# Moving part of three groups' elementwise work from VectorE to GpSimd in an adaLN layer with spectral attention and experts

## The chip, the core and the metric

The kernel runs on one core of a Trainium2 chip. A core has five engines that work through queues of their own and meet at semaphores: TensorE (PE in the profile; PEld are its weight loads), VectorE (DVE), ScalarE (ACT), GpSimd (POOL) and SyncE (SP), which here only issues transfers. The metric is device time in microseconds from the start to the end of one execution; lower is better. Times of several runs are given as a median with the lowest and the highest.

## The reference, cut to what matters

The input `x` has 4 batches of 1024 tokens with 256 features, so 4096 tokens. Everything is float32.

```
sa, ca, ga, sb, cb, gb = parts of silu(c) @ wmod        # one set for each batch
h = layernorm(x) * (1 + ca) + sa
q, k, v = unit_projection(h @ W.T + b)                  # fft, each bin divided by (|f| + 1e-8), ifft
s = cumsum over the tokens of ifft(fft(k) * fft(v))
x = x + ga * ifft(fft(s) * conj(fft(q)))
h = layernorm(x) * (1 + cb) + sb
x = x + gb * experts(h)                                 # top 2 of 8 experts, SwiGLU, 256 -> 512 -> 256
```

`ga` and `gb` are first pushed away from zero. The experts' weights for a token are a softmax over its two best gate values.

## The kernel before, in words

**Groups and pairs.** Tokens are worked in 8 groups of 512 (`GN`), four tiles of 128 tokens each, two groups to a batch. A group's attention is made in two *pairs* of tiles (the generator `pair`), so the first three groups are six pairs. Spectra are held as 256 real numbers: real parts of the bins, then imaginary parts, with bin 0 and the middle bin at the two ends, which have no imaginary part.

**A pair, step by step.** ScalarE normalizes (L503); TensorE turns the tiles (L510) and makes the spectra of k, v and q with the weights folded into the transform (L526); ScalarE copies them out of PSUM into `z` (L533) and squares them into `sq` (L535, L539). The function `magnitudes` then makes the amplitude of each bin in `mag`: GpSimd copies the two end bins (L545), one engine adds the squares of real and imaginary parts (L549), ScalarE takes the root (L550), VectorE adds EPS (L551). It is called once for k and v together (508 elements a partition, the sum on VectorE) and once for q (254 elements, the sum on GpSimd). VectorE multiplies k's and v's amplitudes (L554) and takes the reciprocal (L555); `complex_product` makes the bin product of k and v by two multiplications (L467, L468) and, for real parts, imaginary parts and the last bin, a subtraction, an addition and a copy (L470, L471, L472); L557 scales it. For q VectorE takes the reciprocal (L560) and GpSimd multiplies (L561). TensorE sums over the tokens (L567, L569, L577) into `pc`, with what the pair before left (`sums`, L585). `complex_product` is called again for `pc`, which lies in PSUM, and q; TensorE turns the result (L592) and transforms it back (L602); VectorE adds it to `x` (L610) and takes the moments (L449, L451). Last, ScalarE normalizes into `row` (L629), and VectorE multiplies by `1 + cb` and adds `sb` (L633, L634).

**A group's routing** (`route`): ranks of the gates (L647 to L652, two of these on GpSimd: L649, L650), softmax weights, the slot of each token (up to L708), eight indirect DMAs from GpSimd's queue that scatter `row` into the experts' slots in DRAM (L713), and the write of `x` with the experts' second bias to `out` (L744). GpSimd then refills the token numbers in `row` (L488), once the scatters have read it.

**Expert blocks.** An expert's slots are worked in blocks of 256 tokens (`Block`): rows and first weights are loaded by SyncE (L857, L864), rows turned (L873), 32 products (L910), the gate part on VectorE (L922), ScalarE (L926, L929), VectorE (L932, L933) and GpSimd (L934; VectorE for the blocks planned after the last group), 16 products (L940), the weighting (L950) and two adding DMAs to `out` from GpSimd's queue (L954). `gb` is fetched by indirect DMAs (L893). A block can be worked only when it is sure to be full; the number that is comes from the shapes (`ready`): none after group 0, one after group 1, four more after each of groups 2 to 6, and 18 of the 39 after the last group. A block's load waits for all scatters so far.

**What sets the order.** A loop over steps at the end (L1036 on) advances the generators in turn: a new pair every four steps, eight steps for each, so that two pairs are always under way; routes after their groups; the preparation of the other batches' constants from step 8 on (`prepare_later`); and parts of expert blocks at a rate that spreads those known over the steps. At build time the framework then orders each engine's instructions once for all, from their dependencies and its own estimate of their durations. On the chip each engine takes them in that order, and one that waits holds those behind it.

Of the kernel before, what the change touches and what calls it, by code (L numbers as in the profile page):

```python
# [10 lines left out]
ALU = mybir.AluOpType  # L11
AX = mybir.AxisListType

P = 128
D = 256
# [2 lines left out]
NF = 512  # L18
GT = 4
GN = GT * P  # L20
LATER = 8
PT = 2
ALPHA = 1.702
# [2 lines left out]
EPS = 1e-8  # L26
# [9 lines left out]
def adaln_layer_kernel(  # L36
# [27 lines left out]
    nc = tc.nc  # L64
    NT = x.shape[0]
    BATCH = c_t.shape[2]
    NG = NT // GN
    GPB = NG // BATCH
# [3 lines left out]
    def ready(n):  # L72

        return max(0, -((NE * (BLK - 1) - 2 * n) // BLK))
# [15 lines left out]
    def bank(tag, bufs=1):  # L90
        return ps_m.tile([P, 512], FP, tag=tag, name=tag, bufs=bufs)
# [6 lines left out]
    def load_x(g):  # L98
        t = xpool.tile([P, GT, D], FP, tag="x", name=f"x{g}")
        nc.sync.dma_start(  # L100
            out=t, in_=x[g * GN : (g + 1) * GN, :].rearrange("(i p) d -> p i d", p=P)
        )
# [72 lines left out]
    SB = LOG + NE  # L175
    CB, GB2 = SB + D, SB + 2 * D
# [277 lines left out]
    def bins(t):  # L454

        return t.rearrange("p k (c n) -> p k c n", c=2)

    def sliding(t, at):

        v = t[:, :, at : at + P]  # L460
        return bass.AP(tensor=v.tensor, offset=v.offset, ap=[*v.ap[:2], (1, 2), v.ap[2]])

    def complex_product(a, b, conj):

        u = two.tile([P, PT, D], FP, tag="u", name="u", bufs=3)
        w = two.tile([P, PT, D], FP, tag="w", name="w")
        nc.vector.tensor_mul(bins(u), bins(a), sliding(b, 0))  # L467
        nc.vector.tensor_mul(bins(w), bins(a), sliding(b, NB))  # L468
        re, im = (ALU.add, ALU.subtract) if conj else (ALU.subtract, ALU.add)
        nc.vector.tensor_tensor(u[:, :, 1:P], u[:, :, 1:P], w[:, :, P : D - 1], re)  # L470
        nc.vector.tensor_tensor(u[:, :, P : D - 1], u[:, :, P : D - 1], w[:, :, 1:P], im)  # L471
        nc.vector.tensor_copy(u[:, :, D - 1 :], w[:, :, D - 1 :])  # L472
        return u

    sums = {}
# [18 lines left out]
    def pair(g, j):  # L494

        b, first = g // GPB, g % GPB == 0
        x4, pb = x_tiles[g], of_batch[b]
        root, r, nmr, gate, row = of_group[g]
        xp = x4[:, j : j + PT, :]
        xn = two.tile([P, PT, D], FP, tag="xn", name="xn")  # L500
        for k in range(PT):
# [19 lines left out]
        mag = two.tile([P, PT, 3, P + 1], FP, tag="mag", name="mag")  # L521
# [16 lines left out]
        k_, v, q = (z[:, :, at : at + D] for at in (KV, KV + D, Q))  # L538
# [1 line left out]
        yield  # L540


        def magnitudes(lo, hi, eng):
            for n in range(2):
                nc.gpsimd.tensor_copy(  # L545
                    mag[:, :, lo:hi, n * P : n * P + 1],
                    sq[:, :, lo:hi, n * (D - 1) : n * (D - 1) + 1],
                )
            eng.tensor_add(mag[:, :, lo:hi, 1:P], sq[:, :, lo:hi, 1:P], sq[:, :, lo:hi, P : D - 1])  # L549
            nc.scalar.activation(mag[:, :, lo:hi, :], mag[:, :, lo:hi, :], AF.Sqrt, bias=tiny)  # L550
            nc.vector.tensor_scalar(mag[:, :, lo:hi, :], mag[:, :, lo:hi, :], EPS, None, ALU.add)  # L551

        magnitudes(1, 3, nc.vector)
        nc.vector.tensor_mul(mag[:, :, 1, :], mag[:, :, 1, :], mag[:, :, 2, :])  # L554
        nc.vector.reciprocal(mag[:, :, 1, :], mag[:, :, 1, :])  # L555
        u = complex_product(k_, v, False)
        nc.vector.tensor_mul(bins(u), bins(u), sliding(mag[:, :, 1, :], 0))  # L557
        yield
        magnitudes(0, 1, nc.gpsimd)
        nc.vector.reciprocal(mag[:, :, 0, :], mag[:, :, 0, :])  # L560
        nc.gpsimd.tensor_mul(bins(q), bins(q), sliding(mag[:, :, 0, :], 0))  # L561
        yield
# [2 lines left out]
        pc = bank("mid").rearrange("p (k n) -> p k n", k=PT)  # L565
# [19 lines left out]
        nc.scalar.copy(sums["s"], pc[:, PT - 1, :])  # L585
        yield

        o = complex_product(pc, q, True)
        pt = bank("mid").rearrange("p (h n) -> p h n", h=2)
        for k in range(PT):  # L590
            for h in range(2):
# [35 lines left out]
        h_row = row[:, j : j + PT, :D]  # L627
        for k in range(PT):
# [1 line left out]
                h_row[:, k, :], xp[:, k, :], AF.Identity,  # L630
                bias=nmr2[:, k : k + 1], scale=r2[:, k : k + 1],
            )
        nc.vector.tensor_mul(h_row, h_row, pb[:, CB : CB + D].unsqueeze(1).to_broadcast([P, PT, D]))  # L633
        nc.vector.tensor_add(h_row, h_row, pb[:, SB : SB + D].unsqueeze(1).to_broadcast([P, PT, D]))  # L634
        yield

    def route(g):
# [90 lines left out]
        for i in range(GT):  # L728
            nc.tensor.transpose(pw[:NE, i * P : (i + 1) * P], wt[:, i, :], ident)
        w_t = one.tile([NE, GN], FP, tag="same", name="w_t")  # L730
        nc.scalar.copy(w_t, pw[:NE, :GN])
        for i in range(0, GT, 2):
# [11 lines left out]
        s = nc.sync.dma_start(  # L744
            out=out[g * GN : (g + 1) * GN, :].rearrange("(i p) d -> p i d", p=P), in_=x4
        )
# [97 lines left out]
    class Block:  # L844
# [24 lines left out]
        def turn(self):  # L869
# [31 lines left out]
            self.h = mtwo.tile([P, NF // P, BLK], FP, tag="h", name="h")  # L901

        def hidden(self, pair):
            ps = []
            for s in range(2):
# [130 lines left out]
    for t in range(NG * PER + STEPS - HALFWAY + 3):  # L1036
        if t < NG * PER and t % PER == 0:
            g = t // PER
# [5 lines left out]
        for r in list(routes):  # L1044
            g, step = r[0], r[1]
            next(r[2])
            r[1] += 1
            if step == 2:
                final = g == NG - 1
                count = TOTAL - ready(GN * g) if final else ready(GN * (g + 1)) - ready(GN * g)  # L1050
                if final:
                    fill_tails()
                if count:
                    planned = plan(count, final)
                    eng = nc.vector if final else nc.gpsimd
# [12 lines left out]
        if t < NG * PER and t % HALFWAY == 0:  # L1068
            n = t // HALFWAY
            new = pair(n // PAIRS, n % PAIRS * PT)  # L1070
            pairs.append([n, 1, new])
            next(new)
        if t >= LATER and t % 2 == 0:
            next(later, None)
# [76 lines left out]
```

## Time and profile before

| | us |
|---|---|
| median of 3 runs (lowest to highest) | 825.14 (820.38 to 828.37) |
| the profiled execution, its own time | 821.18 |
| its span | 819.4 |
| TensorE, matmuls | 709.4 (87% of the span) |
| VectorE | 571.8 (70%) |
| ScalarE | 349.8 (43%) |
| GpSimd | 405.2 (49%) |

The mean granted clock of TensorE is 0.928 of full speed. The profile names a group of instructions by line, engine, operation, and the tiles written and read; `x24` is how often it occurs, then come busy time, the mean duration of one in ns, and the idle time of the engine just before such instructions with what ended it. GpSimd's busy time holds the issue of its indirect DMAs.

The first scatters of the groups 0, 1 and 2 start at 99.9, 142.7 and 199.5 us. GpSimd's own elementwise work is small before: per pair it is the end bins, q's sum and q's scaling.

### The profile page before, as it was taken

How to read it: one execution, taken by the hardware profiler on the slowest of the kernel's cores; microseconds unless marked ns; L12 is line 12 of the kernel's file. 1: busy time of each engine (PE TensorE's matmuls, PEld its weight loads, DVE VectorE, ACT ScalarE, POOL GpSimd, SP SyncE). 2: the span in 40 equal slices, each digit the busy share in tenths (PEclk: the TensorE clock that was granted, in tenths of full speed). 3: DMA queues.
4: the chain of work that ended last, by engine and by line, in shares of the span. 5: the costliest groups of instructions: out<-in, count | busy, mean ns of one | idle time of the engine just before them, and what ended most of it. 6: DMA issues, size and time to landing. Idle time of an engine off the chain costs nothing.

```text
span 819.4 us, 10348 instructions
## 1 busy us (share of the span) xinstructions
PE 709.4 (87%) x2980; PEld 548.9 (67%) x2980; DVE 571.8 (70%) x1599; ACT 349.8 (43%) x632; POOL 405.2 (49%) x399
## 2 busy tenths in 40 slices
PE   6989796597697978997999799979889999999994
PEld 5655553364475756775777577748768888888883
DVE  3688979668668676967696759677846666566552
ACT  3444345264364445645564656364122333322320
POOL 1023243515645663665477446745764545454565
PEclk9999998699699999995999699969979999999998
DMA  9300131520761394228422832284687655666631
GB/s 312 126 0 1 63 143 44 179 75 21 215 181 26 82 294 124 38 70 257 104 35 71 256 81 32 74 253 88 175 251 187 151 163 132 174 164 170 157 52 25
DMA packets 57409, 103.33 MB, mean 126 GB/s; under 512 B 7869, under 2 KB 41802, under 8 KB 56842
## 3 DMA queue, kind: packets, MB, share of 16 engines
q1 hardware_dynamic: 39306, 75.32, 26.8%
q0 software_dynamic: 18048, 27.36, 18.8%
q8 instruction: 25, 0.41, 0.2%
q14 instruction: 30, 0.25, 0.1%
HBM read 75.96 MB, written 28.52 MB: 128 GB/s over the span
## 4 chain that ended last, share of the span: by engine, by line
PE 32%; DVE 16%; DMA 9%; issue 8%; ACT 6%; POOL 3%; POOLq 0%; SPq 0%; ACTq 0%; DVEq 0%
PE gv L910 17%; PE py L940 8%; DMA out_dram<-gb,token 3%; DMA x<-in_x_dram 2%; PE in L526 2%; PE late L735 2%; DVE gt L922 2%; ACT L550 1%; DVE vt L933 1%; DVE vt L932 1%; PE turned L873 1%; POOL slots L713 1%; DMA slots<-row,slot_i 1%; POOL out_dram L954 1%; DMA out_dram<-x 1%
## 5 line engine op out<-in xcount | busy, mean ns | idle before, releaser
L910 PE MATMUL gv<-xt,w 128*128 128x256 f32 x1248 | 301.8, 395 | 18.9 <-DVE gt L922 9.7
L910 PEld LDWEIGHTS gv<-xt,w 128*128 128x128 f32 x1248 | 241.9, 198 | 62.8 <-DVE gt L922 11.4
L954 POOL DMA_INDIRECT out_dram<-gb,token x78 | 130.6, 1675 | 41.8 <-DVE gb L950 20.6
L893 POOL DMA_INDIRECT gb<-kept_gb,token x78 | 83.2, 1067 | 132.2 <-DMA out_dram<-gb,token 29.2
L940 PE MATMUL py<-w_sb,h 128*128 x624 | 142.9, 381 | 6.0 <-POOL h L934 5.1
L940 PEld LDWEIGHTS py<-w_sb,h 128*128 128x128 f32 x624 | 118.1, 191 | 22.9 <-POOL h L934 5.5
L926 ACT ACTIVATE sg<-gt 128x512 f32<-128x512 f32 x78 | 49.1, 630 | 178.9 <-DVE gt L922 169.3
L526 PE MATMUL in<-batch,ht 128*128 128x512 f32 (+1 forms) x256 | 95.6, 520 | 6.1 <-ACT ht L514 6.1
L922 DVE TENSOR_SCALAR gt<-gv,bias 128x256 f32<-128x256 f32 x156 | 68.7, 476 | 35.9 <-PE gv L910 35.9
L713 POOL DMA_INDIRECT slots<-row,slot_i x64 | 68.0, 1063 | 41.8 <-DVE slot_i L708 23.2
L934 POOL TENSOR_TENSOR h<-vt,sg 128x512 f32<-128x512 f32 x42 | 55.5, 1322 | 61.5 <-DVE vt L933 35.1
L526 PEld LDWEIGHTS in<-batch,ht 128*128 128x128 f32 x256 | 48.1, 197 | 43.1 <-issue 30.0
L932 DVE TENSOR_SCALAR vt<-vt 128x512 f32<-128x512 f32 x78 | 37.8, 485 | 48.7 <-ACT vt L929 45.4
L929 ACT ACTIVATE vt<-gv,bias 128x256 f32<-128x256 f32 x156 | 64.9, 465 | 9.7 <-PE gv L910 8.8
L933 DVE TENSOR_TENSOR vt<-vt,gt 128x512 f32<-128x512 f32 x78 | 55.4, 711 | 1.8
L545 POOL COPY mag<-sq 128x4 f32<-128x4 f32 (+1 forms) x64 | 19.0, 336 | 69.7 <-ACT sq L535 57.4
L533 ACT COPY z<-in 128x512 f32<-128x512 f32 (+1 forms) x64 | 29.4, 480 | 46.6 <-PE in L526 43.5
L561 POOL TENSOR_TENSOR z<-z,mag 128x512 f32<-128x512 f32 x16 | 21.0, 1312 | 56.0 <-DVE mag L560 46.2
L950 DVE SCALAR_TENSOR_TENSOR gb<-py,weight,gb 128x256 f32<-128x256 f32 x78 | 34.0, 476 | 15.2 <-PE py L940 15.1
L926 ACT ACT_TABLE_LOAD x25 | 32.1, 1283 | 19.9 <-DVE gt L922 18.1
L551 DVE TENSOR_SCALAR mag<-mag 128x516 f32<-128x516 f32 (+1 forms) x32 | 16.0, 501 | 31.8 <-ACT mag L550 31.8
L550 ACT ACTIVATE mag<-mag,tiny 128x516 f32<-128x516 f32 (+1 forms) x32 | 19.6, 619 | 35.0 <-issue 26.4
(212 smaller groups left out, 1014.8 us busy)
## 6 DMA issues: line engine op xcount, KB each, us to landing
w<-in_w1t_dram SPq DMA_DIRECT2D x39, 1024.0 KB
x_in<-slots SPq DMA_DIRECT2D x39, 266.0 KB
x<-in_x_dram SPq DMA_DIRECT2D x8, 512.0 KB
w_sb<-in_w2t_dram SPq DMA_DIRECT2D x1, 4096.0 KB
out_dram<-x SPq DMA_DIRECT2D x8, 512.0 KB
kept<-of SPq DMA_DIRECT2D x2, 1428.0 KB
batch<-kept SPq DMA_DIRECT2D x2, 1428.0 KB
slots<-fill SPq DMA_DIRECT2D x9, 266.0 KB
```

The costliest lines, as they stand in the source:

```text
L526: nc.tensor.matmul(pz, lhsT=ht[:, h, k * P : (k + 1) * P], rhs=pb[:, h * HC + lo : h * HC + hi], start=(h == 0), stop=(h == 1),)
L713: s = nc.gpsimd.indirect_dma_start(out=slots, out_offset=bass.IndirectOffsetOnAxis(ap=slot_i[:, n, i : i + 1], axis=0), in_=row[:, i, :], ...
L893: nc.gpsimd.indirect_dma_start(out=self.gb[:, i, :], out_offset=None, in_=kept_gb, in_offset=bass.IndirectOffsetOnAxis(ap=self.token[:, i, ...
L910: nc.tensor.matmul(pp[:, j, :], lhsT=self.w1[:, h, s, f * P : (f + 1) * P], rhs=self.xt[:, h, :], start=(h == 0), stop=(h == 1),)
L922: nc.vector.tensor_scalar(gt[:, j], ps[0][:, j], self.bias[:, self.k, 0, f : f + 1], LIMIT, ALU.add, ALU.min)
L926: nc.scalar.activation(sg, gt, AF.Sigmoid, scale=ALPHA)
L929: nc.scalar.activation(vt[:, j], ps[1][:, j], AF.Identity, bias=self.bias[:, self.k, 1, f : f + 1])
L932: nc.vector.tensor_scalar(vt, vt, LIMIT + 1.0, 1.0 - LIMIT, ALU.min, ALU.max)
L933: nc.vector.tensor_mul(vt, vt, gt)
L934: self.eng.tensor_mul(self.h[:, 2 * pair : 2 * pair + 2, :], vt, sg)
L940: nc.tensor.matmul(py[:, i, :], lhsT=self.h[:, f, i * P : (i + 1) * P], rhs=w2_sb[:, bass.ds(self.e, 1), f, :].rearrange("p a d -> p (a d) ...
L954: s = nc.gpsimd.indirect_dma_start(out=out, out_offset=bass.IndirectOffsetOnAxis(ap=self.token[:, i, 0:1], axis=0), in_=y[:, i, :], in_off ...
```

## The change

In groups 0, 1 and 2 (`ALONE = 3`) the engine `side` is GpSimd, in the others VectorE as before. `side` makes the sum of squares for k and v, the EPS addition for q, the last three instructions of the bin product of k and v, and the multiplication and addition after the second normalization. All else keeps its engine: the EPS addition for k and v and the whole product of `pc` and q stay on VectorE. Lines after the edit move by one or two. The order of each engine's instructions is made anew and differs from the old one well past the edited groups.

```diff
+ALONE = 3
...
-    def complex_product(a, b, conj):
+    def complex_product(a, b, conj, eng):
...
-        nc.vector.tensor_tensor(u[:, :, 1:P], u[:, :, 1:P], w[:, :, P : D - 1], re)
-        nc.vector.tensor_tensor(u[:, :, P : D - 1], u[:, :, P : D - 1], w[:, :, 1:P], im)
-        nc.vector.tensor_copy(u[:, :, D - 1 :], w[:, :, D - 1 :])
+        eng.tensor_tensor(u[:, :, 1:P], u[:, :, 1:P], w[:, :, P : D - 1], re)
+        eng.tensor_tensor(u[:, :, P : D - 1], u[:, :, P : D - 1], w[:, :, 1:P], im)
+        eng.tensor_copy(u[:, :, D - 1 :], w[:, :, D - 1 :])
...
+        side = nc.gpsimd if g < ALONE else nc.vector
...
-        def magnitudes(lo, hi, eng):
+        def magnitudes(lo, hi, eng, plus):
...
-            nc.vector.tensor_scalar(mag[:, :, lo:hi, :], mag[:, :, lo:hi, :], EPS, None, ALU.add)
-
-        magnitudes(1, 3, nc.vector)
+            plus.tensor_scalar(mag[:, :, lo:hi, :], mag[:, :, lo:hi, :], EPS, None, ALU.add)
+
+        magnitudes(1, 3, side, nc.vector)
...
-        u = complex_product(k_, v, False)
+        u = complex_product(k_, v, False, side)
...
-        magnitudes(0, 1, nc.gpsimd)
+        magnitudes(0, 1, nc.gpsimd, side)
...
-        o = complex_product(pc, q, True)
+        o = complex_product(pc, q, True, nc.vector)
...
-        nc.vector.tensor_mul(h_row, h_row, pb[:, CB : CB + D].unsqueeze(1).to_broadcast([P, PT, D]))
-        nc.vector.tensor_add(h_row, h_row, pb[:, SB : SB + D].unsqueeze(1).to_broadcast([P, PT, D]))
+        side.tensor_mul(h_row, h_row, pb[:, CB : CB + D].unsqueeze(1).to_broadcast([P, PT, D]))
+        side.tensor_add(h_row, h_row, pb[:, SB : SB + D].unsqueeze(1).to_broadcast([P, PT, D]))
```

## The prediction

> **What bounds the kernel now.** I read the page's busy time in 40 slices first, then busy time by stage, then the chain that ended last, the groups of instructions, and the timelines of VectorE (DVE) and GpSimd (POOL).
>
> ```profile
> PE   6989796597697978997999799979889999999994
> DVE  3688979668668676967696759677846666566552
> POOL 1023243515645663665477446745764545454565
> ```
>
> A digit is 20.5 us. In the first ten slices DVE is mostly at 6 to 9 and POOL at 0 to 5; from slice 29 on PE is full and stays full. The stages, cut where their work changes (columns: stretch, length, then busy us and counts of PE, weight loads, DVE, ACT, POOL, then granted clock, DMA share, GB/s):
>
> ```profile
> 33.00:143.00 110.00, 90.01 (x328) 57.87 (x327) 96.47 (x258) 51.16 (x97) 32.70 (x49) 0.95 0.12 47
> 143.00:159.00 16.00, 11.31 (x28) 5.71 (x27) 14.62 (x57) 3.52 (x8) 9.97 (x11) 0.70 0.38 116
> 159.00:172.00 13.00, 9.35 (x39) 7.92 (x40) 4.21 (x15) 4.68 (x9) 1.42 (x2) 0.74 0.76 257
> 172.00:212.00 40.00, 28.27 (x96) 16.89 (x94) 34.17 (x114) 19.84 (x37) 17.96 (x24) 0.85 0.08 28
> 212.00:590.00 378.00, 333.06 (x1376) 256.57 (x1377) 280.64 (x802) 196.39 (x331) 220.12 (x210) 0.92 0.49 130
> 590.00:819.00 229.00, 211.96 (x1000) 183.75 (x998) 128.44 (x287) 63.01 (x133) 120.72 (x88) 0.97 0.57 148
> ```
>
> Groups 0 and 1 and most of group 2's first steps run from 33 to 143 us. There DVE is busy 96.5 of 110 us (88%) and POOL 32.7 (30%): DVE sets the pace. From 159 to 172 DVE waits for the first expert block's weights (DMA 76% busy). From 212 to 590 PE works 88% and DVE 74%, groups and experts mixed. After 590 PE alone counts. The change touches nothing after group 2, so it pays only by bringing the start of the later stages forward. That start shows in the chain:
>
> ```profile
> 208.90 2.49 DMA slots<-row,slot_i
> 212.45 6.15 DMA w<-in_w1t_dram
> 218.74 3.69 PE gv L910 x16
> ```
>
> The chain begins with group 2's last scatter: SyncE's queue can't load the next blocks before it. What group 2's scatter gains, the end gains, if the later order repeats itself.
>
> **What the Trainium skill says.** (1) "SBUF — State Buffer", section "Who interferes with whom": a DVE instruction with two SBUF inputs and a GpSimd instruction that reads SBUF exclude one another, for a whole instruction. The timelines agree (start, length):
>
> ```profile
> 130.77 1.23 POOL L561 TENSOR_TENSOR z<-z,mag 128x512 f32<-128x512 f32 x1 [5.92 <-DVE mag L560]
> 131.26 1.28 DVE L633 TENSOR_TENSOR row<-row,batch 128x512 f32<-128x512 f32 x1 [0.64 <-ACT row L629]
> 154.85 1.22 POOL L561 TENSOR_TENSOR z<-z,mag 128x512 f32<-128x512 f32 x1
> 155.08 1.53 DVE L634 TENSOR_TENSOR row<-row,batch 128x512 f32<-128x512 f32 x1
> ```
>
> L633 and L634 take 0.68 us as a rule; here they end about 0.54 us after POOL does. (2) "GPSIMD Engine Reference", section "Engine selection": two-input elementwise work is about twice as slow as on DVE, one-input work about at line rate. The trace agrees on the first: 1228 ns (L561, 512 elements) against some 680 for DVE's like. (3) The same page has POOL without access to PSUM; the product that reads PSUM, `pc` times `q`, indeed keeps its engine.
>
> **The change, part by part.** Rows used, from the groups by shape between 33 and 215 us:
>
> ```profile
> L561 POOL TENSOR_TENSOR z<-z,mag 128x512 f32<-128x512 f32 x8 | 9.8, 1228 | 37.0 <-DVE mag L560 27.1 <-DVE gate L621 9.9
> L549 POOL TENSOR_TENSOR mag<-sq 128x254 f32<-128x254 f32 x8 | 6.0, 754 | 0.0
> L549 DVE TENSOR_TENSOR mag<-sq 128x508 f32<-128x508 f32 x8 | 5.4, 680 | 0.0
> L470 DVE TENSOR_TENSOR u<-u,w 128x254 f32<-128x254 f32 x15 | 6.2, 413 | 0.0
> L551 DVE TENSOR_SCALAR mag<-mag 128x258 f32<-128x258 f32 x8 | 2.3, 283 | 0.0
> ```
>
> DVE instructions overlap their ends, so what one frees is the step from its start to the next start in the timeline: L549 0.60 us, L470 and L471 0.33 each, L472 0.07, the small L551 0.20, L633 and L634 0.60 each. Every pair of tiles in the first three groups loses all of these on DVE: 2.73 us; six pairs, 16.4 us.
>
> POOL gains per pair: L549 of 508 elements, 1.22 us (between the 254- and 512-element rows, nearly the latter); L470 and L471 at 0.72 (the median of POOL's L549 of the same size); L472 at 0.16 (half of a two-copy L545, 0.31); L633 and L634 at 1.23 each. L551 of 258 elements with one input has no row: from 0.37 (line rate by the skill's page at its 1.2 GHz, 0.22, plus the 0.15 of a tiny copy) to 0.75 (a two-input op of that size); I take 0.45. Neither end can be below nothing. Sum 5.7 us per pair, 34 us in all. POOL has that room (32.7 of 110 busy), so its throughput is no bound; its place in the chains and its lock on the shared port are.
>
> *To group 1's scatter (142.7 us).* By then the freed steps are L549 six times (3.6), L470 to L472 of the bin product five times (3.65), the small L551 five times (1.0), L633 and L634 of four pairs (4.8): 13.0 us of DVE.
>
> *The lock.* Between 33 and 212 us, eight DVE instructions last over 0.25 us longer than their form usually does, each beside a POOL operation: 6.2 us together. POOL's two-input operations there sum to about 20.6 us (eight L561, eight L549, six L649 and L650). So a POOL microsecond costs DVE 0.30. Added two-input work by 142.7 us: 6 x 1.22 + 5 x 1.44 + 4 x 2.46 = 24.4 us, so 7.3 us lost. Bounds: none, since the operations that leave DVE are themselves mostly two-input ones and what stays (reciprocals of 1.75 us, statistics, PSUM reads) doesn't lock; or 0.5 per us, 12.2 lost, which would be each operation meeting one in mid-course. I keep 7.3.
>
> *The waits.* I walked both queues from 33 us on in the new order, which differs from the old one. Before, DVE's sum ran ahead of ScalarE's square root (L550) with the k-v product's tail to do in between; now POOL makes the sum, ScalarE takes the root, and DVE reaches L551 with that tail gone. Pair 0: about 0.9 us later. Pair 2: POOL must first do L633 and L634 of pair 0 (2.5 us) and then the 1.22 us sum; queued behind DVE's L551 are the output product's last three instructions and with them PE's transposes (L592). DVE waits 3.6 us there, where 2.0 are lost today. At the ranking of group 0, POOL has a pair's 1.22 us sum ahead of L649: 0.8 us more. Against that, group 0's eight scatters (10.3 us of POOL) now stand behind L561 of pair 3, not ahead of it, so DVE's L467 no longer waits for them: about 1.5 back. Net about 1.8 us lost.
>
> So group 1's scatter comes 13.0 - 7.3 - 1.8 = 3.9 us earlier.
>
> *From there to group 2's scatter.* The load wait of 159 to 172 us keeps its length and moves along. Freed after it: L633 and L634 of pair 5, 1.2 us; of pair 4 (154 us) and the product's tail of pair 5 nothing counts, since DVE then idles anyway (1.9 us more gain if that wait were gone). POOL pays: pair 5's L551 now stands behind group 1's scatters, then L488, L633 and L634 precede L561; that chain has the load wait as cover, and would cost 2.5 us without it. Ahead of the ranking of group 2 (L649, whose result DVE's L652 waits for) POOL does L633 and L634 and then L561: about level with today's 191 us. But the expert's L934 comes behind, 2.7 us later, and PE's L940 with it, about 1 us on the path to L708, after the lock's share of 0.7. Net -0.5: 1.2 - 1.0 - 0.7.
>
> No DMA is added, and SyncE's queue moves by an order only: one output write behind a block's loads.
>
> Sum: 3.4 us, taken as 3.5. From the profiled execution's 821.2 us (819.4 span and 1.8 around it) that gives 817.7; this execution lies 4.0 below the median of the runs, so against 825.1 I forecast 821.6.
>
> **The rivals.**
> *A. The lock hardly costs* (0.05 per us, 1.2 lost) and the waits of pairs 0 and 2 are filled. For it: POOL's L561 at 44.1, 59.4 and 74.8 us cost DVE nothing, beside statistics and PSUM reads. Against it: the eight long instructions counted above. Gain 13.0 - 1.2 - 0.5, less 0.5 after: 10.8; 814.
>
> *B. Slower: POOL's queue comes ahead of DVE's.* POOL's order is fixed; L633 and L634 with their wait on ScalarE (L629) stand ahead of the next pair's sum, so DVE's L551 waits in each pair as at pair 2, and PE, idle longer, loses clock (0.70 in 143 to 159 us already). Price: 2.5 us, the length of L633 and L634 on POOL, in each of six pairs, 15 us; against 16.4 freed less 34 x 0.3 = 10.2: 9 us slower, 834. It decides from a wait of 1.0 us per pair ((16.4 - 10.2) / 6). For it: the new order has this queueing in pairs 2, 4, 5. Against it: DVE has other pairs' work and the setup of batches ahead of most of those waits.
>
> *C. The time is given back.* Groups 3 to 7 get another order through the shift; the x loads and w1 loads (10.8 and 6.2 us in the chain) set the pace there, and the gain to 212 us is lost by 590: 825. The change itself can't fail to take place: the instruction lists show the six pairs' operations on POOL.
>
> **How the numbers follow.** Forecast (gain 1 to 7 us) 0.48, A 0.18, B 0.17, C 0.17. One per cent, 8.25 us, is about what a measurement of this kernel can tell from no change. Faster by over that: most of A and a tail of the forecast, 0.21. Slower: most of B, 0.14. Within: 0.65. The range from 813 to 832 holds A's centre, with the lock at nothing or the waits gone at its lower end, and reaches to 2 us short of B's 834; outside are B's worse half and the tail of A, 2 in 10.
>
> **What would show it.** POOL busy up by about 34 us and DVE down by some 20 (durations, not steps, less the lock's excess); group 1's first scatter at about 139 us and group 2's at about 196; between 33 and 143 us DVE instructions longer than their form by 7 us more. A is right if that excess doesn't grow; B if DVE's waits at L551, L557 and L560 for ScalarE and POOL sum to 10 us more; C if the scatter of group 2 is earlier and 590 us is not. It would be wrong if POOL's 508-element sum took far more than 1.3 us, or if DVE and POOL blocked each other in chains.

## The result, and the profile after

The change makes the kernel slower: 834.96 us in the median (833.58 to 836.42) against 822.89 us (820.38 to 828.37) for the kernel before beside it. The ratio is 1.0136, 95% interval 1.0106 to 1.0165. The profiled execution took 836.42 us, its span is 834.6 us; its mean granted clock is 0.915, against 0.928 in the profiled execution before.

The busy time in 40 slices, of 20.9 us each here:

```profile
PE   6988787788499868997998799979979999999994
DVE  3596878758657674896599649876946665666552
POOL 1344456724635653475657555655765445454555
```

In slices 2 to 7 GpSimd (POOL) is at 3 to 6 where it was at 0 to 4, as meant. VectorE (DVE) is hardly lower there, and TensorE (PE) is about as busy as before. By stage, with the columns of the prediction's table:

```profile
33.00:143.00 110.00, 90.21 (x318) 58.66 (x316) 87.26 (x200) 46.28 (x88) 57.61 (x76) 0.94 0.12 47
143.00:159.00 16.00, 8.01 (x25) 5.31 (x26) 14.23 (x60) 5.24 (x12) 11.21 (x16) 0.71 0.11 42
159.00:172.00 13.00, 8.24 (x15) 3.71 (x15) 6.48 (x26) 4.32 (x9) 9.15 (x10) 0.50 0.61 194
172.00:212.00 40.00, 35.07 (x130) 24.41 (x128) 29.90 (x102) 21.87 (x39) 15.26 (x20) 0.90 0.17 58
```

From 33 to 143 us GpSimd did 24.9 us more and VectorE 9.2 us less, yet the work got less far: the first scatters of groups 0, 1 and 2 moved from 99.9, 142.7 and 199.5 to 108.1, 151.8 and 208.2 us. Group 0's, before and after:

```profile
99.91 1.18 POOL L713 DMA_INDIRECT slots<-row,slot_i  x1 [13.47 <-DVE slot_i L708]
```

```profile
108.14 1.24 POOL L715 DMA_INDIRECT slots<-row,slot_i  x1 [3.79 <-DVE slot_i L710]
```

So some 8 us are gone before group 0's scatter, and the rest of the head only carries them along. A second loss comes later. The scatter of group 3 is 10.2 us late, that of group 4 16.5 us late, and from there the shift stays (14.6 us at group 7). The chain that ended last passes through that place:

```profile
221.10 6.31 DMA w<-in_w1t_dram
...
311.33 8.96 DMA out_dram<-x
320.35 6.83 DMA x<-in_x_dram
329.32 5.79 PE in L528 x8
```

The first line answers to the prediction's weights at 212.45 us, now 8.7 us later. The last three stand at the second loss: a load of `x` waits for an earlier write, and TensorE's products wait for the load.

### The profile page after: what moved, and what is told of

The parts are those of the page before. It is cut to its first block, busy times and chain, and to the rows that moved or that the text cites. A ratio compares the mean times of both kernels' runs of the same rounds, so it can differ in the third digit from the quotient of the medians.

```text
span 834.6 us, 10354 instructions
## 1 busy us (share of the span) xinstructions
PE 720.4 (86%) x2980; PEld 555.6 (67%) x2980; DVE 565.1 (68%) x1557; ACT 351.8 (42%) x634; POOL 442.0 (53%) x441
## 4 chain that ended last, share of the span: by engine, by line
PE 47%; DVE 23%; ACT 10%; issue 7%; DMA 6%; POOL 6%; SPq 0%; POOLq 0%; DVEq 0%; ACTq 0%
PE gv L912 20%; PE py L942 9%; PE in L528 5%; POOL slots L715 3%; PE late L737 2%; DVE vt L935 2%; DVE gt L924 2%; ACT L552 2%; DMA slots<-row,slot_i 1%; DVE mag L562 1%; PE turned L875 1%; ACT mag L552 1%; DVE vt L934 1%; ACT L928 1%; DMA out_dram<-gb,token 1%
## 5 line engine op out<-in xcount | busy, mean ns | idle before, releaser
L912 PE MATMUL gv<-xt,w 128*128 128x256 f32 x1248 | 302.0, 395 | 12.9 <-ACT xn L505 4.0
L528 PE MATMUL in<-batch,ht 128*128 128x512 f32 (+1 forms) x256 | 99.4, 532 | 4.0 <-ACT ht L516 3.2
L547 POOL COPY mag<-sq 128x4 f32<-128x4 f32 (+1 forms) x64 | 17.1, 305 | 66.8 <-ACT sq L537 57.5
L553 DVE TENSOR_SCALAR mag<-mag 128x516 f32<-128x516 f32 (+1 forms) x26 | 15.4, 591 | 36.0 <-ACT mag L552 36.0
```

The costliest lines, as they stand in the source:

```text
L528: nc.tensor.matmul(pz, lhsT=ht[:, h, k * P : (k + 1) * P], rhs=pb[:, h * HC + lo : h * HC + hi], start=(h == 0), stop=(h == 1),)
L912: nc.tensor.matmul(pp[:, j, :], lhsT=self.w1[:, h, s, f * P : (f + 1) * P], rhs=self.xt[:, h, :], start=(h == 0), stop=(h == 1),)
```

## The experiments

All ratios below are to the kernel before, run beside each kernel. Traces are one execution each. That of the kernel before (821.18 us) lies 3 to 6 us under its medians in the later comparisons (824.5 to 827.3). So ends are read from the ratios, and small delays only between kernels with one order.

### The parts one by one, and ScalarE's queue

The first three runs put one part on GpSimd each and leave the order to the framework, which makes it anew each time:

```diff
+        magnitudes(1, 3, side, nc.vector)
...
+        u = complex_product(k_, v, False, side)
...
+        side.tensor_mul(h_row, ...
+        side.tensor_add(h_row, ...
```

The first line alone is in e1, the last two in e2, the second in e3; the other operations stay where they were.

> Only the sum of squares for k and v is on GpSimd in groups 0 to 2; product tail, EPS and the second normalization stay on VectorE. Theory Q (queues): the loss comes from GpSimd standing between the squares and ScalarE's square root, with ScalarE's copies of q's spectra and so TensorE held behind the waiting root. Then this edit alone is slower than before by 5 to 9 us (828 to 832 against 823), and group 0's scatter is 4 us or more later than 99.9 us. Theory L (lock): the loss is VectorE blocked by GpSimd's two-input operations, in proportion to these; this edit has 1.2 of the 5.2 us per pair and frees 0.6 us of VectorE per pair, so the time stays within 2 us of before.

> Only the multiplication and addition after the second normalization are on GpSimd in groups 0 to 2. Theory Q: nothing but the scatter waits for them, 1.2 us of VectorE per pair is freed, so 2 to 6 us faster than before (817 to 821). Theory L: they are 2.4 of the 5.2 us of two-input work per pair, so they carry half of the loss of 12 us: 3 to 6 us slower than before (826 to 829).

> Only the last three instructions of the k-v product are on GpSimd in groups 0 to 2. Theory Q: their result is wanted only after VectorE's reciprocal of 1.75 us, which covers them; 0 to 4 us faster than before. Theory L: 1.4 of the 5.2 us of two-input work, so 2 to 4 us slower than before.

Measured: the sum alone 1.0038 (1.0014 to 1.0061), the rows alone 1.0163 (1.0087 to 1.024), the product's tail alone 0.9936 (0.9914 to 0.9958). Against the kernel before beside them, none of the three lies where either theory put it. The rows, which looked harmless, were the worst, though their figure is the least certain: it rests on four executions between 827.27 and 844.65 us.

The fourth run keeps the whole change and orders ScalarE's root for k and v behind the copies and squares of q's spectra, since in the change's trace those copies stood queued behind a root that waited for GpSimd:

```diff
-            nc.scalar.activation(mag[...], mag[...], AF.Sqrt, bias=tiny)
+            rt = nc.scalar.activation(mag[...], mag[...], AF.Sqrt, bias=tiny)
+            if lo and g < ALONE:
+                tc.add_manual_dep(rt.ins, q_sq.ins.name, ORDER, reason='copies first')
```

> The changed kernel, with ScalarE's root for k and v ordered behind its copies and squares of q (L535, L541) in groups 0 to 2, an order within ScalarE's queue and no further wait. Theory Q: while the root waits for GpSimd's sum, TensorE gets its banks back, so part of the 8 us by group 0's scatter returns: 828 to 832, that scatter at 104 us or earlier. Theory L: no change from 835 by more than 2 us.

Measured: 0.9972 (0.9952 to 0.9992), so 1.6% regained. That looked like proof of the theory of ScalarE's queue. It was not: the framework had remade every engine's order around this one edit.

### Holding the order still

Instructions have the same names whichever engine takes them. So the order of one build can be written into another as dependencies that order and don't wait:

```diff
+ORDER = mybir.DependencyInfo(mybir.DependencyClass.NoSync, mybir.DependencyReason.DATA)
+KEPT = (
...
+    made = {i.name: i for i in nc.cur_bb.bb.instructions}
+    last_of = {}
+    for code in KEPT.split():
+        i = made.get(f"I-{int(code, 36)}")
...
+        if i.engine in last_of:
+            tc.add_manual_dep(i, last_of[i.engine], ORDER, reason="kept order")
+        last_of[i.engine] = i.name
```

`KEPT` lists another build's instructions in its sequence; each engine then takes its own in that sequence. This separates what the change moves from what the framework makes of it. Four such kernels come first: the change in the old order, the kernel before in the change's order, and two parts in the old order. No run kept a kernel's own order with nothing else altered; the nearest is h1 below, with five instructions moved.

> All the work of the change stays on GpSimd, but every engine takes its instructions in the order that the kernel before had (moved instructions stand on GpSimd where they stood in the old sequence as a whole). Three theories. O, the remade order is the loss: moving the work is by itself worth about nothing or a little, so the ratio to the kernel before is 0.990 to 1.002. E, the moved work itself is the loss (GpSimd later with the sum and the rows than VectorE was, and the shared port): 1.008 to 1.018, as the change itself (1.0136). Q, a part of O: what costs is ScalarE's square root waiting for GpSimd's sum with the copies of q's spectra behind it; the old order has those copies ahead of the root in pair 2, so 0.993 to 1.003, and group 0's first scatter within 4 us of 99.9 rather than at 108.

> No work is moved: all stays on the engines of the kernel before, but every engine takes its instructions in the order that the change brought about. O: the order alone carries the loss, ratio 1.008 to 1.016, and the 6 to 7 us lost between 300 and 325 us are there again. E: 0.995 to 1.003. Q: the head of the run is not late, since VectorE makes the sum early and ScalarE's root doesn't wait; only the later part of the loss (group 4, 6 to 7 us) may remain, so 0.998 to 1.008.

> Only the second normalization's multiply and add on GpSimd, in the old order. With the order left to itself this part was slower by 1.6% in few runs (interval 0.9 to 2.4%). O: that came from the order (TensorE took the next pair's products behind the wait for the gates of the next batch at 110 us, and stood 2.8 us there), so here 0.992 to 1.002. E: GpSimd's rows stand ahead of the ranks and hold the routing of groups 0 and 1, 1.005 to 1.015.

> Only the sum of k's and v's squares on GpSimd, in the old order. With the order left to itself it was slower by 0.38% (0.14 to 0.61%). O: 0.994 to 1.001. E and Q: GpSimd takes 1.26 us for what VectorE takes 0.68, and ScalarE's root waits for it at each pair with what stands behind, 1.002 to 1.008 whatever the order.

Measured: 1.0248 (1.0194 to 1.0302), 1.0067 (1.0042 to 1.0093), 1.0131 (1.0087 to 1.0174) and 1.0073 (1.0047 to 1.01). The second figure decides. O as the whole loss falls, and so does E: the order alone carries 0.67%, about half. It lies in Q's range, which h1 below tests. The other half, 1.0136 over 1.0067 or 0.7% (some 0.3 to 1.1 with both intervals), is the moved work in the change's own order. In the old order it costs still more, so this split belongs to the change's order.

With one order in two traces, each instruction's delay can be followed. In the change's order, from the kernel before to the change, group 0's scatter goes from 101.7 to 108.1 us, group 1's from 144.6 to 151.8 and group 2's from 201.6 to 208.2: the moved work loses 6.4 us by 108 us and then nothing more. Followed on VectorE the delay is 0.6 us at 33 us, before anything moved, and grows by 0.6 us in pair 0, 0.5 in pair 1, 1.9 in pair 2, 1.3 at group 0's ranking and 1.6 right after it. Pair 2 is the largest. First the timelines of ScalarE and VectorE of the kernel before in the change's order, then those of GpSimd, ScalarE and VectorE of the change (start, length, in brackets idle time and what ended it):

```profile
62.36 0.73 ACT L550 ACTIVATE mag<-mag,tiny 128x516 f32<-128x516 f32 x1 [0.94 <-POOL mag L545]
63.38 0.42 DVE L551 TENSOR_SCALAR mag<-mag 128x516 f32<-128x516 f32 x1
```

```profile
64.68 1.26 POOL L551 TENSOR_TENSOR mag<-sq 128x508 f32<-128x508 f32 x1
65.98 0.73 ACT L552 ACTIVATE mag<-mag,tiny 128x516 f32<-128x516 f32 x1 [2.83 <-POOL mag L551]
66.61 0.64 ACT L535 COPY z<-in 128x264 f32<-128x264 f32 x2
66.73 0.43 DVE L553 TENSOR_SCALAR mag<-mag 128x516 f32<-128x516 f32 x1 [2.20 <-ACT mag L552]
```

VectorE made this sum at 61.58 us, right after the rows (60.25 and 60.97). GpSimd makes it at 64.68 us, since it has first the rows of pair 0 (62.02 to 64.48 us); the root is 3.6 us later, and so are the copies behind it (66.61 for 62.99 us); VectorE's EPS addition is 3.4 us later. TensorE stands idle for these copies, 3.39 us against 1.19 in the kernel before in the change's order, and its next products in the change's trace are slow:

```profile
67.02 0.66 PE L512 MATMUL in<-msk,xn 128*128 128x128 f32 x4 [3.39 <-ACT z L535]
67.52 1.76 PE L342 MATMUL mid<-gmat,rows_of 128*128 128x256 f32 x4
69.07 1.91 PE L346 MATMUL mid<-fwd,bb 128*128 128x256 f32 x4
```

In the other trace each of these two groups took 1.03 us. The granted clock is 0.50 from 67.8 to 71.0 us here and 1.00 from 64.0 to 67.4 us there, and VectorE's L348 then waits 1.72 us for these products. So a part of pair 2's 1.9 us is TensorE's clock. The ranking loses its time in GpSimd's queue again: GpSimd does a sum (81.99 us) ahead of the ranks, and VectorE's reduction L654 waits for them. The last 1.6 us are TensorE's. Its products for the next batch's gates, in the kernel before in the change's order and in the change:

```profile
85.06 1.13 PE L341 MATMUL late<-gmat,rows_of 128*128 128x256 f32 x4 [2.61 <-DVE batch L397]
```

```profile
89.93 2.08 PE L342 MATMUL late<-gmat,rows_of 128*128 128x256 f32 x4 [3.89 <-DVE batch L398]
```

After an idle time of 2.61 us the four products took 1.13 us, after 3.89 us they took 2.08, and the next two groups 1.91 and 1.75 where they took 1.03 and 1.10 in the other trace. The wait cost a second time. The Trainium skill, page "TensorE: Matmul & The Clock Gate", section "Part 1: The HAM clock gate", says that TensorE falls to half its clock after an idle window of about 3.4 us and needs about as long to come back. This place agrees: the granted clock is 1.00 from 84 to 88 us in the first trace and 0.50 from 88.2 to 94.9 us in the second. But 3.4 us is no sharp limit for one idle time in these traces: the first has the clock at 0.50 from 101.2 to 104.4 us after an idle time of 2.84 us.

What the order costs by itself comes elsewhere. The time from group 3's scatter to group 4's is 89.6, 89.0 and 87.8 us in the three kernels with the change's order (the change, h1 below, f2), and 82.8 to 85.8 us in the other seventeen. VectorE and TensorE of the kernel before in the change's order, then in its own:

```profile
321.29 0.43 DVE L449 BATCH_NORM_STATS2 st<-x 128x6 f32<-128x256 f32 x1 [2.47 <-DMA x<-in_x_dram]
322.19 0.87 PE L592 MATMUL mid<-msk,u 128*128 128x128 f32 x4 [1.91 <-DVE u L470]
```

```profile
311.15 0.60 PE L592 MATMUL mid<-msk,u 128*128 128x128 f32 x4
317.65 1.41 DVE L449 BATCH_NORM_STATS2 st<-x 128x6 f32<-128x256 f32 x4 [5.41 <-DMA x<-in_x_dram]
```

In the new order VectorE has the first statistics of the newly loaded `x` ahead of the tail of a pair's output product (L470 to L472). So this tail waits for the load, and with it TensorE's turning L592 and the 16 products queued behind it. In the old order the tail and the products come first. This place wasn't mended alone, so its price isn't measured alone.

### ScalarE's root by itself

The change in its own order, with five places of the root on ScalarE moved and nothing else (`KEPT` is a list of numbers; the lines stand for them here):

```diff
-    L552 (k and v), L535 (q), L541 (q)
+    L535 (q), L541 (q), L552 (k and v)
```

> The change with its own order on every engine but ScalarE, where in pairs 0 to 4 the root of k's and v's squares stands behind the copies and squares of q's spectra instead of ahead of them. Q, ScalarE's held queue is the loss: 8 to 12 us back, ratio to the kernel before 0.998 to 1.004. O, the gain of the run with remade orders came from other places of the order: 1.009 to 1.016, as the change (1.0136).

Measured: 1.011 (1.0073 to 1.0147), which can't be told from the change's 1.0136: with both intervals, nothing to 0.7% came back. Group 0's scatter came only from 108.1 to 106.0 us: in pair 2 q's copy came 2.1 us earlier, but in pairs 0 and 1 the later root held VectorE (its EPS addition 1.8 and 2.9 us later). So Q is not the whole loss. What it carries of the 0.7% isn't settled, and most of e4's 1.6% came with the other engines' orders.

### Orders without the moved work

The kernel before, in the orders of e4 and of e3; last, the whole change in e3's order. Only `KEPT` differs.

> No work moved, in the order of the run whose root stands behind q's copies (0.9972 with the work moved). O, that order is good by itself and the moved work still costs as it does in the change's order (0.7%): 0.988 to 0.993. Q, the order only takes away the wait that the moved sum brings, and the moved work is then about neutral: 0.996 to 1.003.

> No work moved, in the order of the run with only the product's tail on GpSimd (0.9936). C, the tail's 0.73 us of VectorE per pair is the gain: 0.998 to 1.003. O, the order is the gain: 0.991 to 0.996, and moving the tail is worth nothing.

> All the moved work on GpSimd, in the order that was best so far with no work moved (0.9924). The moved work costs there what it cost in the change's own order, 0.7%, or in the other, 0.25%: 0.994 to 1.001. If it stands worse in GpSimd's queue, as in the old order (rows ahead of ranks, a sum behind the ranks): 1.003 to 1.012. Below 0.992 the change would pay in this order, and the theory that it never does would fall.

Measured: 0.9947 (0.9926 to 0.9968), 0.9924 (0.9898 to 0.9951), 0.9956 (0.9927 to 0.9985). The first lies between its two expectations, the second in O's range, the third in the range where the moved work costs 0.25 to 0.7%. Side by side, from the measured ratios:

| order of | no work moved | work moved | difference |
|---|---|---|---|
| the kernel before | 1 | 1.0248 (all) | +2.5% |
| the change | 1.0067 | 1.0136 (all) | +0.7% |
| e4 | 0.9947 | 0.9972 (all) | +0.25% |
| e3 | 0.9924 | 0.9956 (all) | +0.3% |
| e3 | 0.9924 | 0.9936 (tail alone) | +0.1% |

With each pair's intervals taken together the last three differences can't be told from nothing (about 0.3 to 0.4 either way), the first two can. In no order did moving the work gain. And four orders of one and the same work span 1.4%, as much as the whole loss. The gain of e3 was its order (O, not C); what makes that order better stays open. The lowest ratio of the kernels that do all the work is that of the one before with e3's order kept, which moves none of it: 820.66 us beside 826.63.

The tail on GpSimd in all eight groups, order left free:

```diff
-        u = complex_product(k_, v, False, side)
+        u = complex_product(k_, v, False, nc.gpsimd)
```

> The product's last three instructions on GpSimd in all eight groups, order left to itself. C: from group 3 on TensorE works 88% of the time and VectorE's chain of a pair is covered by expert work, so it adds little to the 0.9936 of three groups: 0.990 to 0.996. If VectorE's time counts there as well: five groups times two pairs times 0.73 us, 7 us more, 0.984 to 0.988.

Measured: 1.0039 (1.0016 to 1.0061), outside both expectations. Group 2's scatter to group 3's took 77.9 us, against 71.8 in e3. Whether order or work did that wasn't separated.

### GpSimd's queue: one small copy among the scatters

The tail alone in the old order, and then the same with the copy L473 of pair 3 moved ahead of group 0's scatters on GpSimd:

```diff
-    L471, L472, L715 x7, L473, L715
+    L471, L472, L473, L715 x8
```

> Only the product's last three instructions on GpSimd, in the old order (0.9936 with the order left to itself). C: on VectorE they stand in the pair's own chain between the multiplications and the EPS addition, and on GpSimd they run beside the root and the reciprocal; 4 to 6 us faster whatever the order, 0.992 to 0.997, unless they stand among group 0's scatters on GpSimd, where in the old order they were late by some 9 us with everything moved: then 1.000 to 1.010. O, the gain of that run was its order: 0.999 to 1.003.

> The tail alone on GpSimd in the old order (1.0087), with one change: in pair 3 the last copy of the product (two elements a tile) stands ahead of group 0's eight scatters in GpSimd's queue, not among them. If the queue is the loss, VectorE's scaling of the product comes 9 us earlier at 101 us and the ratio is 0.992 to 0.999; if not, 1.006 to 1.011 again.

Measured: 1.0087 (1.0062 to 1.0112) and 0.9991 (0.9965 to 1.0016). GpSimd and VectorE, first with the copy among the scatters, then ahead of them:

```profile
110.04 0.21 POOL L473 COPY u<-w 128x2 f32<-128x2 f32 x1
110.28 0.69 DVE L559 TENSOR_TENSOR u<-u,mag 128x512 f32<-128x512 f32 x1 [7.70 <-issue]
```

```profile
93.66 0.19 POOL L473 COPY u<-w 128x2 f32<-128x2 f32 x1
102.52 0.68 DVE L559 TENSOR_TENSOR u<-u,mag 128x512 f32<-128x512 f32 x1
```

A copy of 0.2 us behind seven scatters of 1.3 us each held VectorE for 7.7 us. The trace names no releaser for the first wait, but the two kernels' orders differ in this one instruction alone, and 0.96% came back. In f1, the change in the old order, the same copy stands among the scatters, and VectorE waits 7.92 us for it; so its 2.5% holds this loss too.

### The rows, and what freed VectorE time is worth

In f3, the rows on GpSimd in the old order, the ranking of group 1 waits (GpSimd's timeline, then VectorE's):

```profile
136.43 1.19 POOL L636 TENSOR_TENSOR row<-row,batch 128x512 f32<-128x512 f32 x1
137.56 0.74 POOL L651 TENSOR_TENSOR ranks<-ranks,msk 128x256 f32<-128x256 f32 x1
...
139.13 0.42 DVE L654 TENSOR_REDUCE rank<-ranks 128x32 f32<-128x256 f32 x1 [2.18 <-POOL ranks L652]
```

The kernel before started this reduction at 135.25 us, after a wait of 0.17. So I put each group's rows behind its ranks (`KEPT`: L651, L652, then both pairs' L635 and L636).

> The rows' multiply and add on GpSimd as in the run with the rows alone in the old order (1.0131), but each group's four such instructions stand behind that group's two instructions for the ranks, and ahead of its scatters. N, GpSimd's queue is the loss: in that run VectorE's reduction of the ranks came 2.0 us later in group 1 and 2.5 us later in group 2 because the rows stood ahead of the ranks; they come back, 1.003 to 1.009. S, the loss is the shared port and the slower instructions wherever they stand: 1.011 to 1.016. If the rows now hold the scatters instead, the scatters come 1 to 3 us later than the slots are known.

Measured: 1.0103 (1.0051 to 1.0154), between N and S and not to be told from f3. The ranks do come sooner, but the rows now run beside the routing's short instructions (GpSimd, then VectorE):

```profile
140.25 1.71 POOL L635 TENSOR_TENSOR row<-row,batch 128x512 f32<-128x512 f32 x1
...
140.84 1.14 DVE L680 TENSOR_TENSOR earlier<-earlier,chosen 128x8 f32<-128x8 f32 x1
```

L680 takes 0.15 us in the kernel before; here it ends with GpSimd's row. Group 1's scatter is at 150.8 us, later than with the rows ahead of the ranks (146.6; 1.2 us of that are there before any work of the edit). How much of the 1.0% comes from such meetings isn't measured.

Two runs ask what the freed time would bring if nothing were put on GpSimd. In the old order, the first leaves out nearly all of the rows' two instructions, the second nearly all that the change moves:

```diff
+        n = 1 if g < ALONE else D
+        h_part = h_row[:, :, :n]
-        nc.vector.tensor_mul(h_row, h_row, ...
-        nc.vector.tensor_add(h_row, h_row, ...
+        nc.vector.tensor_mul(h_part, h_part, ...
+        nc.vector.tensor_add(h_part, h_part, ...
```

The second has besides this:

```diff
-            eng.tensor_add(mag[:, :, lo:hi, 1:P], sq[:, :, lo:hi, 1:P], sq[:, :, lo:hi, P : D - 1])
-            nc.scalar.activation(mag[:, :, lo:hi, :], mag[:, :, lo:hi, :], AF.Sqrt, bias=tiny)
+            n = 2 if lo and g < ALONE else P
+            eng.tensor_add(mag[:, :, lo:hi, 1:n], sq[:, :, lo:hi, 1:n], sq[:, :, lo:hi, P : P + n - 1])
+            nc.scalar.activation(mag[:, :, lo:hi, :], (sq if n == 2 else mag)[:, :, lo:hi, : P + 1], AF.Sqrt, bias=tiny)
+            m = 1 if not lo and g < ALONE else P + 1
+            nc.vector.tensor_scalar(mag[:, :, lo:hi, :m], mag[:, :, lo:hi, :m], EPS, None, ALU.add)
...
-        u = complex_product(k_, v, False)
+        u = complex_product(k_, v, False, 2 if g < ALONE else P)
```

> The kernel before in its own order, but in groups 0 to 2 the second normalization's multiply and add on VectorE touch one column of 256 instead of all (the scaling and shift of those rows is left out, so the experts' inputs differ; the instruction count is the same). This asks what the freed VectorE time is worth when nothing is put on GpSimd for it. D, VectorE sets the pace of the head, as the prediction had it: 4 pairs times 1.0 us by group 1's scatter and 1 to 2 more by group 2's, so 4 to 6 us faster, ratio 0.992 to 0.995. C, each pair's chain across the engines sets the pace and the rows lie beside it: the freed time turns into idle time of VectorE, 0.998 to 1.001.

> The kernel before in its own order, with all that the change moves left out in groups 0 to 2 but for one column or bin each: the sum of k's and v's squares (the root then takes the real parts' squares alone), the EPS addition for q, the last three instructions of the product of k and v, and the multiply and add of the rows. Values differ from the reference from there on; instruction counts are the same and nothing is put on GpSimd. Some 14 us of VectorE are freed. D, VectorE sets the pace: 12 to 15 us faster, 0.981 to 0.986. C, the freed time mostly turns into idle time, but the sum and the tail also lie in each pair's own chain: 4 to 9 us, 0.989 to 0.995.

Measured: 0.9961 (0.9943 to 0.9979) and 0.9878 (0.9838 to 0.9917). The rows' twelve instructions fell from 0.69 to 0.16 us, 6.4 us in all; the kernel gained 825.98 x 0.0039 = 3.2 us. Leaving out everything freed some 14 us (six pairs at the prediction's 2.73, less about 0.4 for what remains) and gained 827.29 x 0.0122 = 10.1 us (6.9 to 13.4), which decides between neither expectation; the rows' figure lies between theirs too. Freed time counts, but not in full: in the second trace VectorE's idle time from 33 to 143 us is 20.7 us, against 14.1 before. Part of the second gain may be the shorter chain of each pair, in which the sum and the tail lie; that wasn't separated.

## Why the prediction was wrong

**The sum.** Forecast a gain of 3.5 us, measured a loss of 822.89 x 0.0136 = 11.2 us: 14.7 us apart. Of these 5.5 us (0.67%) are the new order. The other 9.2 us are the moved work, which costs some 5.7 us where 3.5 were to be gained. The total lands on rival B's 834 by luck: only about half of it is B's mechanism.

**Right: what moves and what it does to the shared port.** GpSimd's busy time rose by 36.8 us (34 forecast). Take the kernel before in the change's order (f2) and the change, each from its first L467 or L468 (32.6 and 33.1 us) to group 1's scatter (144.6 and 151.8 us). The time by which VectorE's instructions there exceed the usual length of their form (its tenth percentile) grew from 8.1 to 15.4 us, by 7.2; forecast were 7.3. In the change 19 of them are over 0.25 us too long, each beside a GpSimd instruction; in f2 there are 7. VectorE's total fell by only 6.7 us, not 20: the page counts overlapping instructions once, so that about the 16.4 us of steps could go, and the longer instructions take part of that back.

**Wrong first: the waits.** The step "Net about 1.8 us lost" failed. Between the same two kernels and in the same stretch VectorE's idle time grew from 12.9 to 24.5 us, by 11.6. The sum then closes: 11.6 us of idle time and 7.2 of longer instructions, in a stretch that became 6.6 us longer, leave 12.2 us freed, near the 13.0 counted. So the freed time and the shared port were sized about right, and the waits were not. Part of the 11.6 us is freed time that nothing filled: the step of 13.0 us took every freed microsecond for a gain, and left out alone the rows brought half of theirs. The rest are waits. Pair 0 cost 0.6 us, less than the 0.9 forecast, and pair 2 1.9 us where I put 1.6; but these are what is left after the freed time, which I had booked as gain. At pair 2 I named what queues behind VectorE's L551, and not what queues behind ScalarE's L550 and GpSimd's L549. Pair 1 (0.5 us) had no term, and TensorE's slow products (1.6 us after the ranking, and some in pair 2) had none outside rival B. From group 1's scatter to group 2's the moved work lost nothing, where I had 0.5.

**Wrong second: the order taken as neutral.** I wrote that the gain to group 2's scatter would reach the end "if the later order repeats itself", saw that the order was remade far past group 2, and gave it no term of its own. Rival C came near the place (loads of `x`), but as a delay that eats a gain, not as an order that costs 5.5 us even with nothing moved.

**Small terms.** A GpSimd row of the change, by shape, from 33 to 215 us:

```profile
L553 POOL TENSOR_SCALAR mag<-mag 128x258 f32<-128x258 f32 x6 | 5.8, 958 | 3.2 <-ACT mag L552 3.2
```

I took 0.45 us for this EPS addition, with 0.75 as the upper end; it took 0.96 in the mean (0.87 to 0.89 in five of the six). The "about line rate" for one-input work, on which the prediction's lower end of 0.37 us rests, doesn't hold here. Six of them are 3 us of GpSimd, but they stand on q's chain. The sum of 508 elements, in the row beside it, took 1.40 us for my 1.22.

**Rival B**, as put, priced 2.5 us of waiting in each of six pairs. In the change's order such waits came in pairs 0 to 2 and at the ranking, 4.3 us net, part of which in pair 2 is TensorE's clock, and after them 1.6 us of that clock, whose loss B names. With the old order held still, the rows and the sum on GpSimd, each alone, cost 1.3 and 0.7% (f3, f4). That fits B, but doesn't tell its queueing from the shared port: with the rows behind the ranks (g2) the loss can't be told from f3's.

## What to carry to other kernels

Moving an instruction to an idle engine is priced by the chain it stands in and the queue it joins, not by the busy time it frees: ask what waits for its result, what stands ahead of it on the new engine, and what stands behind each engine that now waits. Where a framework makes the order, each edit draws a new one, and here orders of the same work differed by 1.4%, as much as the edit itself; hold the order still before you call a gain or a loss the edit's own. A good order found by accident can be kept without the edit that found it.

## What was not expected of the hardware

A one-input GpSimd operation is not cheap: 0.96 us in the mean for 258 elements, against 0.28 us on VectorE, and above the 0.75 us of a two-input GpSimd operation of 254 elements. A VectorE instruction of 8 elements that starts beside a GpSimd two-input operation of 512 lasts until about when that ends (1.14 us for 0.15), so beside GpSimd work a short instruction in a serial chain can take many times its own length. The copy of 0.2 us that held VectorE for 7.7 us shows the like for queues: GpSimd's eight scatters are one block of some 10 us to whatever stands among them.
